# Two-layer graph network on one Trainium2 core: the opening loads in another order, one of them in another buffer, and other landing times in the plan

## The chip, the cores and the metric

The kernel runs on one core of one Trainium2 chip. The metric is device time in microseconds (us), lower is better. Beside the timed runs there is one profiled execution, from which every duration below is taken.

## What is computed

The input `x` holds 64 graphs of 256 nodes with 256 features, `adj` their 256 x 256 adjacency matrices (int32). Two layers follow each other.

```
# layer 0, with g = gat(h, W, a):
#   Wh = h @ W; e = leaky_relu(Wh @ a[:256] + (Wh @ a[256:]).T, 0.2)
#   g  = softmax(where(adj > 0, e, -9e15), axis=1) @ Wh
h = gat(gat(x, W1, a1), W2, a2)
h = layernorm(x + h, g_ln1, b_ln1)
x = layernorm(h + relu(h @ w_ff1 + b_ff1) @ w_ff2 + b_ff2, g_ln2, b_ln2)
# layer 1: eight heads of 32, attention weights masked by relation r and summed over r
A = softmax(q @ k.T / sqrt(32))
o = sum_r (A * (adj == r)) @ v_r
x = layernorm(x + o @ Wo + bo, g1, beta1)
x = layernorm(x + gelu(x @ W1 + b1) @ W2 + b2, g2, beta2)
```

Everything is fp32. The mask of layer 0 is 0 or 1, so that `adj` doubles as the mask of relation 1 in layer 1.

## The kernel before

The 64 graphs are worked on in 32 pairs. For each pair `whole_way` runs `gat_layers` (two graph attention layers), `feed_forward`, `attention` and a second `feed_forward`. Up to four pairs and a generator of one-time work, `reliefs` (it folds biases into each other and forms sums of weight blocks), are interleaved.

**A plan written by a simulator inside the kernel.** `run` keeps a clock for each engine (first values in `START`) and a time for each buffer (`free`). TensorE's work comes in steps that the generators yield, other engines' work in pieces handed over by `put` with a cost in us. The piece that could begin first is emitted, and `keep_order` ties each engine's instructions into that order. So the plan's guesses of when something lands change only the ORDER on each engine; what the chip waits for are the real semaphores. Loads that were issued before `run` starts enter the plan as fixed times: the dictionary `landed` (first normalisation's weights `ln0`, feed-forward weights `ff0` and `ff1`, `attention` weights) and the second argument of `load`.

**Engines work in order.** A DVE (VectorE) instruction that waits for a load holds everything behind it on DVE. SP (SyncE) issues nearly all loads, one queue, in order, and its waits hold the loads behind them too. The build gives each DMA one of eight completion semaphores in turn, so that SP issues a load only when the eighth load before it has landed.

**The opening.** Loads for the folded weight w12 come first (`W2`, `W1T`, `a2`, `a1c`). TensorE forms w12 (L127), DVE copies it out (L130). Then, for pair 0: products of `xT` with w12 (L528), evacuations (L520), exponentials (L451 to L453), transposes of their rows (L464) and copies (L467), attention weights `e` on DVE (L499, L501, L504), scaling of the node rows by the reciprocal sums on ACT (L509), the products of the first graph layer (L544), the same again for the second layer, with products L557. L570 adds the residual rows `x`, `layernorm` follows. The adjacency of a pair is read twice, by ACT, which makes bytes of it (L303, `small_adj`), and by DVE, which takes its maximum (L307, `largest`).

**Buffers.** `xT` and `adjT` share one buffer named `input`. For the first two pairs only, `adjT` goes into a buffer named `v` instead, which layer 1 uses later for its values: each of the two asks the pool for a tile `v` of which there is one, and takes half of it. The pool lets a new tile `v` be written when all readers of the one before have finished. `qk` is layer 1's buffer of queries and keys, also a single one.

**One-time work on DVE that waits for loads.** L899 adds a bias to each of three normalisation biases (`biased`), L901 subtracts weights (`differences`). The third addition of L899 reads `b_L_gnn_beta`, 42nd in SP's list. L912 and L921 are `reliefs`' products on TensorE, L340 the sums of weight blocks on DVE.

Of the kernel before, what the change touches and what calls it, by code (L numbers as in the profile page):

```python
# [10 lines left out]
F32 = mybir.dt.float32  # L11
# [7 lines left out]
P = 128  # L19
# [6 lines left out]
EVEN = 1e-37  # L26
HURRIED = 2
SLACK = 0.3
START = {"tensor": 8.5, "vector": 8.0, "scalar": 4.0, "gpsimd": 0.0, "sync": 32.0}


@with_exitstack
def two_layers(ctx: ExitStack, tc: tile.TileContext, t: dict, out: bass.AP, flag: bass.AP):
# [15 lines left out]
    KC = D // P  # L49
# [10 lines left out]
    io = ctx.enter_context(tc.tile_pool(name="io", bufs=1))  # L60
# [18 lines left out]
    def weights(name, pool=const):  # L79
        w = t[name]  # L80
        kc, m = w.shape[0] // P, w.shape[1]
        s = pool.tile([P, kc, m], F32, name="w_" + name)
        nc.sync.dma_start(s, w.rearrange("(c p) m -> p c m", p=P))
        return s
# [8 lines left out]
    def column(name):  # L93

        s = const.tile([P, t[name].shape[1]], F32, name="c_" + name)
        nc.sync.dma_start(s, t[name])
        return s

    work = ctx.enter_context(tc.tile_pool(name="work", bufs=1))
# [4 lines left out]
    def bank():  # L104
        return psum.tile([P, 512], F32, name="ps")
# [23 lines left out]
    for m in range(KC):  # L129
# [8 lines left out]
               "gpsimd": mybir.EngineType.Pool, "sync": mybir.EngineType.SP}  # L138
    clock = dict(START)
    waiting = {engine: [] for engine in engines if engine != "tensor"}  # L140
    alone = {}
    free = {name: [0.0] * n for name, n in (("bank", 8), ("a", 2 * HQ), ("m", 2 * HQ), ("h", 2 * HQ), ("yb", 1), ("yT", 2), ("yTa", 1),
                                             ("input", 1), ("rows", 1), ("e", 2), ("adj", 4), ("sums_yT", 1), ("sums_yTa", 1), ("x", 4))}
    table, moved = [None], [START["sync"]]

# [28 lines left out]
    def frees_at(time, names):  # L174
        for name in names:
            free[name].append(time)
# [9 lines left out]
    def takes(needs, count=1):  # L186
        for _ in range(count if needs else 0):
            free[needs].remove(min(free[needs]))

    def at_time(us):  # L190
        event = Event()
        event.time = us
        return event
# [83 lines left out]
        return slice(2 * b, 2 * b + 2)  # L277


    def load(pair, at=None):  # L280


        to, rows = {}, slice(2 * pair, 2 * pair + 2)

        def adjT():
            if at is not None:
                to["adjT"] = work.tile([P, 2, 2, 2 * D], F32, name="v")[:, pair].bitcast(I32).rearrange(
                    "p b (c n) -> p (b c) n", c=2)
            else:
                to["adjT"] = io.tile([P, 4, N], I32, name="input")  # L290
            nc.sync.dma_start(to["adjT"], t["adjT"][rows].rearrange("b (c p) n -> p (b c) n", p=P))

        def xT():
            to["xT"] = io.tile([P, KC, 512], F32, name="input")
            nc.sync.dma_start(to["xT"], t["xT"][pair].rearrange("(c p) b n -> p c (b n)", p=P))

        def x():
            to["x"] = io.tile([P, 4, D], F32, name="x", bufs=4)
            nc.sync.dma_start(to["x"], t["x"][rows].rearrange("b (c p) d -> p (b c) d", p=P))

        def small_adj():
            to["adj"] = io.tile([P, 4, N], U8, name="adj", bufs=4)
            nc.scalar.activation(to["adj"], to["adjT"], AF.Copy)  # L303

        def largest():
            to["empty"] = small.tile([P, 4], F32, name="empty", bufs=4)
            nc.vector.tensor_reduce(most[:, pair], to["adjT"].bitcast(U32), axis=AX.X, op=ALU.max)  # L307
            nc.vector.tensor_scalar(to["empty"], most[:, pair], 0.0, EVEN, ALU.is_le, ALU.mult)

        def in_bytes(there):  # L310
            return put("vector", 1.35, largest, put("scalar", 1.2, small_adj, there, needs="adj", rank=2), rank=2)

        def there(emit, *after, **more):
            return put("sync", 0.45, emit, *after, rank=3, lag=2.3, kb=512, **more)

        if at is None:
            adj = in_bytes(there(adjT, needs="input"))
            return to, [there(xT, adj), adj, there(x, needs="x")]
        takes("input", pair == 0)
        takes("x")  # L320
        for emit in (xT, adjT, x):
            emit()
        return to, [at_time(at), in_bytes(at_time(at)), at_time(at)]

    def first_weights(name, wide=None):

        w = t[name]
        rows = w.shape[1] // 2  # L330
        s = const.tile([P, 7, rows], F32, name="w_" + name)
        for c, at in ((0, (0, 2)), (1, (1, 6))):
            for half, n in enumerate(at):
                nc.sync.dma_start(s[:, n], w[c * P:(c + 1) * P, half * rows:(half + 1) * rows])
        return s
# [179 lines left out]
    def gat_layers(pair, to, loads):  # L515
        yield loads[:1], ["gat"], 2
        y = work.tile([P, 4, D + 4], F32, name="xw", bufs=2)

        def evacuated(to, k, wide, ps):
            return put("scalar", 0.4, lambda: nc.scalar.activation(to[:, k, :wide], ps[:, :wide], AF.Copy),  # L520
                       took(0.88), frees=["bank"])

        there = []
        for b in range(2):
            for j in range(2):
                k, ps = 2 * b + j, bank()
                for c in range(KC):
                    nc.tensor.matmul(ps[:, :D + 4], lhsT=to["xT"][:, c, k * P:(k + 1) * P], rhs=w12[:, c],  # L528
                                     start=c == 0, stop=c == KC - 1)
                there.append(evacuated(y, k, D + 4, ps))  # L530
            if b == 0:
                yield [], None, 2
        frees_at(clock["tensor"], ["input"] * (pair > 0))
        at_home, ratio, there = yield from addends(y, there, D + 2, 0, pair)
        e = [gat_weights(y, D + 2, at_home, ratio, [loads[1], *there], to, b) for b in range(2)]
        there = []
        for b in range(2):
            yield [e[b][1], *([] if b or not pair else [through_gat[pair - 1]])], None, 2
            if b == 0:
                z = work.tile([P, 4, D + 4], F32, name="xw", bufs=2)  # L540
            for i in range(2):
                ps = bank()
                for j in range(2):
                    nc.tensor.matmul(ps[:, :D + 2], lhsT=e[b][0]["e"][:, j, i * P:(i + 1) * P], rhs=y[:, 2 * b + j, :D + 2],  # L544
                                     start=j == 0, stop=j == 1)
                there.append(evacuated(z, 2 * b + i, D + 2, ps))
            frees_at(clock["tensor"], ["e"])
        done_with("gat")
        at_home, ratio, there = yield from addends(z, there, D, 1, pair)
        e = [gat_weights(z, D, at_home, ratio, there, to, b) for b in range(2)]  # L550
        normal = {}
        for b in range(2):
            yield [e[b][1], loads[2]], None, 1
            ps = bank()
            for i in range(2):
                for j in range(2):
                    nc.tensor.matmul(ps[:, i * D:(i + 1) * D], lhsT=e[b][0]["e"][:, j, i * P:(i + 1) * P],  # L557
                                     rhs=z[:, 2 * b + j, :D], start=j == 0, stop=j == 1)
            there = took(1.73)
            frees_at(there.time, ["e"])  # L560
            added = add_rows(to["x"], ps, b, there, loads[2])
            transposed(to["x"], layernorm(to["x"], ln[0], b, added, biased[0]), normal, b, pair, 0)
        happens(through_gat[pair], clock["tensor"])
        return normal
# [305 lines left out]
    def layernorm_weights(g, beta, more=None):  # L870
        if more:
            passing = work.tile([P, 2, 512], F32, name="ff", bufs=NF // 2)[:, 0, :D]
            v = t[more]
            nc.sync.dma_start(passing, bass.AP(tensor=v.tensor, offset=v.offset, ap=[[0, P], [1, D]]))
            more = passing, column(more + "c")
        return on_all(g, D), on_all(beta, D), more

    landed = {name: at_time(us) for name, us in (("ln0", 8.0), ("ff0", 15.0), ("attention", 30.0), ("ff1", 37.0))}
    loaded = {0: load(0, 6.5)}
    ln = [layernorm_weights("L0_gnn_g_ln1", "L0_gnn_b_ln1", "L0_gnn_b_ff2")]  # L880
    ff0 = (first_weights("L0_gnn_w_ff1p"), column("L0_gnn_b_ff1"), weights("L0_gnn_w_ff2"))
    loaded[1] = load(1, 18.0)
    ln.append(layernorm_weights("L0_gnn_g_ln2", "L0_gnn_b_ln2", "L1_gnn_bo"))

    wqk, wv = (const.tile([P, 7, D], F32, name=n) for n in ("wqk", "wv"))
# [11 lines left out]
    ff1 = (first_weights("L1_gnn_W1p"), column("L1_gnn_b1"), weights("L1_gnn_W2"))  # L897
# [502 lines left out]
```

## Time and profile before

| | us |
|---|---|
| four runs | 3042.93, 3044.46, 3045.43, 3047.18 |
| median | 3044.95 |
| profiled execution, its own time | 3047.15 |
| its span on the core | 3045.4 |

| engine | busy us | share of the span |
|---|---|---|
| TensorE matmul (PE) | 2997.9 | 98% |
| VectorE (DVE) | 2555.2 | 84% |
| ScalarE (ACT) | 1752.9 | 58% |
| GpSimd (POOL) | 253.6 | 8% |

PE is busy nearly throughout, in all slices of the span but the first and the last. So time is found or lost where PE is idle or its clock is lowered, and both happen in the first 65 us. The share of busy time over the whole span tells nothing of that stretch; it is read from the timeline, the chain of waits and windows of 2 us. `PEclk` in a window is the TensorE clock that was granted, 1.00 being full.

### The profile page before, as it was taken

The page shows a single profiled execution, that of the slowest core. Times are in us where ns is not written, and L with a number is a line of the kernel's source. Part 1 is how long each engine was busy: PE and PEld are TensorE (multiplying, and loading weights), DVE is VectorE, ACT ScalarE, POOL GpSimd, SP SyncE. Part 2 cuts the span into 40 slices and gives each one's busy share as a digit, 9 for nine tenths or more (in the row PEclk, how much of TensorE's full clock was granted, in tenths as well). Part 3 has the DMA queues.
Part 4 walks back from the last instruction along what each step waited for, and adds up shares of the span by engine and source line. Part 5 has one row for each costly group of instructions (what it writes and reads, how often), then busy time and mean ns, then how long its engine had stood idle before and what let it go on. Part 6 is the DMA issues. An engine that isn't in the chain of part 4 may idle for free.

```text
span 3045.4 us, 52870 instructions
## 1 busy us (share of the span) xinstructions
PE 2997.9 (98%) x19146; PEld 2454.6 (81%) x19146; DVE 2555.2 (84%) x5993; ACT 1752.9 (58%) x4096; POOL 253.6 (8%) x518
## 2 busy tenths in 40 slices
PE   7999999999999999999999999999999999999998
PEld 6887788878888888888888888888888888788876
DVE  5888988788988888888889888889888898888875
ACT  4556666556556555555565565565555655555654
POOL 0100010001100001100001000011000011000100
PEclk8999999999999999999999999999999999999999
DMA  6211141212212222112222112221122221122100
GB/s 182 77 47 60 35 125 56 70 57 82 69 42 67 77 84 77 53 53 70 84 84 77 39 60 77 84 77 61 50 69 80 84 77 52 54 70 70 50 1 22
DMA packets 211147, 205.76 MB, mean 68 GB/s; under 512 B 22336, under 2 KB 170432, under 8 KB 210880
## 3 DMA queue, kind: packets, MB, share of 16 engines
q1 hardware_dynamic: 210464, 202.06, 20.9%
q8 instruction: 153, 2.51, 0.3%
q14 instruction: 114, 0.93, 0.1%
q10 hardware_dynamic: 416, 0.26, 0.0%
HBM read 137.51 MB, written 64.73 MB: 66 GB/s over the span
## 4 chain that ended last, share of the span: by engine, by line
PE 68%; DVE 22%; DMA 5%; ACT 2%; issue 1%; SPq 1%; POOL 0%; DVEq 0%; ACTq 0%; POOLq 0%
PE ps L712 22%; PE ps L681 17%; PE ps L825 5%; PE ps L759 5%; PE ps L754 5%; DVE x L598 4%; PE ps L544 4%; PE ps L796 3%; DVE h L837 3%; PE ps L557 2%; DMA home<-yb 2%; PE ps L847 2%; DVE st L582 2%; DVE m L807 2%; PE ps L528 2%; DVE ff L392 2%
## 5 line engine op out<-in xcount | busy, mean ns | idle before, releaser
L712 PE MATMUL ps<-w_L_gnn_w_ff,ff 128*128 128x256 f32 x2048 | 470.9, 381 | 0.0
L712 PE MATMUL ps<-w_L_gnn_W,ff 128*128 128x256 f32 x2048 | 456.1, 380 | 1.8 <-ACT ff L693 1.8
L593 ACT ACTIVATE x<-x,less,rstd 128x256 f32<-128x256 f32 x512 | 279.1, 596 | 294.4 <-POOL less L589 294.2
L712 PEld LDWEIGHTS ps<-w_L_gnn_w_ff,ff 128*128 128x128 f32 x2048 | 386.6, 190 | 61.5 <-issue 9.8
L712 PEld LDWEIGHTS ps<-w_L_gnn_W,ff 128*128 128x128 f32 x2048 | 388.2, 190 | 57.6 <-ACT ff L693 2.6
L588 POOL TENSOR_TENSOR rstd<-rstd,mhalf 128x2 f32<-128x2 f32 x256 | 198.7, 776 | 2763.0 <-DVE less L585 2630.6
L807 DVE TENSOR_TENSOR m<-a,adj 128x512 f32<-128x512 f32 x512 | 349.0, 682 | 57.9 <-ACT a L803 57.9
L803 ACT ACTIVATE a<-ps 128x512 f32<-128x512 f32 x512 | 267.9, 603 | 222.9 <-PE ps L796 222.8
L681 PE MATMUL ps<-yT,w_L_gnn_W1p 128*128 128x256 f32 x1280 | 315.2, 382 | 4.7 <-ACT ff L687 2.4
L392 DVE TENSOR_TENSOR ff<-ps,ff 128x512 f32<-128x512 f32 x384 | 262.3, 684 | 65.6 <-PE ps L681 57.4
L681 PE MATMUL ps<-yT,w_L_gnn_w_ff1p 128*128 128x256 f32 x1280 | 307.5, 381 | 4.7 <-ACT ff L687 4.1
L687 ACT ACTIVATE ff<-ps 128x512 f32<-128x512 f32 x384 | 223.8, 590 | 98.1 <-PE ps L681 97.7
L681 PEld LDWEIGHTS ps<-yT,w_L_gnn_W1p 128*128 128x128 f32 x1280 | 240.2, 190 | 48.1 <-ACT ps L835 8.5
L681 PEld LDWEIGHTS ps<-yT,w_L_gnn_w_ff1p 128*128 128x128 f32 x1280 | 240.8, 190 | 46.8 <-ACT ff L687 14.3
L837 DVE RECIPROCAL h<-ps 128x256 f32<-128x256 f32 x128 | 223.3, 1745 | 21.6 <-PE ps L828 21.2
L509 ACT ACTIVATE xw<-xw,rs 128x258 f32<-128x258 f32 (+1 forms) x256 | 115.9, 502 | 201.6 <-DVE rs L504 201.5
L693 ACT ACTIVATE ff<-ff,c_L_gnn_b_ff 128x256 f32<-128x256 f32 x384 | 171.6, 504 | 94.4 <-DVE ff L392 94.2
L693 ACT ACTIVATE ff<-ff,c_L_gnn_b 128x256 f32<-128x256 f32 x384 | 173.2, 501 | 84.4 <-DVE ff L392 83.2
L811 DVE TENSOR_TENSOR h<-a 128x256 f32<-128x256 f32 x512 | 212.8, 416 | 0.0
L582 DVE BATCH_NORM_STATS2 st<-x 128x6 f32<-128x256 f32 x512 | 205.7, 402 | 0.9
L570 DVE TENSOR_TENSOR x<-ps,x 128x512 f32<-128x512 f32 x256 | 169.9, 680 | 16.2 <-PE ps L712 9.2
L769 ACT ACTIVATE qk<-ps,bqk 128x256 f32<-128x256 f32 x256 | 106.8, 469 | 111.3 <-PE ps L754 111.0
(128 smaller groups left out, 5011.2 us busy)
## 6 DMA issues: line engine op xcount, KB each, us to landing
home<-yb SPq DMA_DIRECT2D x182, 256.0 KB, 2.0
yT<-home SPq DMA_DIRECT2D x728, 64.0 KB, 2.0
rows<-row SPq DMA_DIRECT2D x60, 512.0 KB, 4.1
input<-in_xT SPq DMA_DIRECT2D x32, 512.0 KB, 4.8
x<-in_x SPq DMA_DIRECT2D x32, 512.0 KB, 4.0
out<-x SPq DMA_DIRECT2D x32, 512.0 KB, 5.1
input<-in_adjT SPq DMA_DIRECT2D x30, 512.0 KB, 4.4
v<-in_adjT SPq DMA_DIRECT2D x2, 512.0 KB, 6.8
```

The costliest lines, as they stand in the source:

```text
L392: nc.vector.tensor_tensor(self.target(c, h), self.bank[bank], self.target(c, h), ALU.add)
L582: nc.vector.bn_stats(st[:, j, :], rows[j])
L588: nc.gpsimd.tensor_tensor(rstd, rstd, mhalf[:, :2], ALU.pow)
L593: nc.scalar.activation(rows[j], rows[j], AF.Identity, bias=less[:, j:j + 1], scale=rstd[:, j:j + 1])
L681: nc.tensor.matmul(to, lhsT=w1[:, a, (t + slab) * P:(t + slab + 1) * P], rhs=b, **flags)
L687: return put("scalar", 0.5, lambda: nc.scalar.activation(target(c, h), blocks.bank["x"], AF.Copy), event, rank=-1)
L693: evacuated[h][m] = put("scalar", 0.4, lambda m=m, to=to, source=source: nc.scalar.activation(to, source, func, bias=b1[:, m:m + 1]), even ...
L712: nc.tensor.matmul(p2[:, j * D:(j + 1) * D], lhsT=f[m][:, (2 * j + b) * P:(2 * j + b + 1) * P], rhs=w2[:, m, :], start=m == 0, stop=m == N ...
L803: nc.scalar.activation(a[n][o], ps[o], AF.Exp)
L807: nc.vector.tensor_tensor(m[n][o], a[n][o], adj, ALU.mult)
L811: nc.vector.tensor_tensor(h[n][o], a[n][o][:, :N], a[n][o][:, N:], ALU.add)
L837: there = put("vector", 1.68, lambda: nc.vector.reciprocal(s, po[:, N:]), there, rank=0)
```

## The change

The first numbers of the plan change (`START`, `landed`, the arguments of `load`), which moves instructions on PE, DVE and ACT. In SP's queue the second pair's `xT` and `adjT` move ahead of the feed-forward weights, the two residual tiles `x` move behind them: `x` of pair 0 to just before `w_ff1p`, `x` of pair 1 to just after `w_ff2`. The second pair's `xT` is loaded into a tile `qk`, so that it no longer shares `input` with the first pair's. `x` is now emitted later than the rest of its load, by a list `rest`; each load has a time of its own in the plan.

```diff
-START = {"tensor": 8.5, "vector": 8.0, "scalar": 4.0, "gpsimd": 0.0, "sync": 32.0}
+START = {"tensor": 11.5, "vector": 11.5, "scalar": 4.0, "gpsimd": 0.0, "sync": 36.0}
...
+    rest = []
...
         def xT():
-            to["xT"] = io.tile([P, KC, 512], F32, name="input")
+            if at is not None and pair == 1:
+                to["xT"] = work.tile([P, 2, KC, 512], F32, name="qk")[:, 0]
+            else:
+                to["xT"] = io.tile([P, KC, 512], F32, name="input")
...
-        for emit in (xT, adjT, x):
+        for emit in (xT, adjT):
             emit()
-        return to, [at_time(at), in_bytes(at_time(at)), at_time(at)]
+        rest.append(x)
+        return to, [at_time(at[0]), in_bytes(at_time(at[1])), at_time(at[2])]
...
-        frees_at(clock["tensor"], ["input"] * (pair > 0))
+        frees_at(clock["tensor"], ["input"] * (pair != 1))
...
-    landed = {name: at_time(us) for name, us in (("ln0", 8.0), ("ff0", 15.0), ("attention", 30.0), ("ff1", 37.0))}
-    loaded = {0: load(0, 6.5)}
+    landed = {name: at_time(us) for name, us in (("ln0", 13.0), ("ff0", 23.0), ("attention", 35.0), ("ff1", 41.0))}
+    loaded = {0: load(0, (8.0, 9.5, 16.0))}
     ln = [layernorm_weights("L0_gnn_g_ln1", "L0_gnn_b_ln1", "L0_gnn_b_ff2")]
+    loaded[1] = load(1, (14.0, 15.5, 25.0))
+    rest[0]()
     ff0 = (first_weights("L0_gnn_w_ff1p"), column("L0_gnn_b_ff1"), weights("L0_gnn_w_ff2"))
-    loaded[1] = load(1, 18.0)
+    rest[1]()
```

## The prediction

> **What bounds the kernel now.** I read the page first. PE is busy 98% of the span; only its first slice (76 us) is thin. So at most what is lost in that slice can come back.
>
> ```profile
> span 3045.4 us, 52870 instructions
> PE   7999999999999999999999999999999999999998
> PEclk8999999999999999999999999999999999999999
> ```
>
> Second, the chain of waits in order of time, for the first 140 us: it names what PE waited for.
>
> ```profile
> 6.65 5.25 PE ps L127 x16
> 11.90 5.47 PE ps L528 x16
> ...
> 34.67 5.95 DMA b_L_gnn_beta<-in_L_gnn_beta
> ...
> 40.72 0.43 DVE b_L_gnn_beta L899
> ...
> 45.05 5.97 PE ps L557 x16
> 51.02 0.87 PE ps L464 x8
> 51.89 1.68 PE ps L912 x16
> 53.57 1.83 PE ps L921 x8
> 55.41 3.46 PE ps L912 x32
> 58.87 5.28 PE ps L544 x16
> ```
>
> From 45.05 on the chain stays on PE without a break. Before that it hangs on the load of beta, issued at 34.67 and landed 5.95 us later, at 40.62: DVE stands in L899 for it, pair 0's second weights `e` (L499) stand behind L899, and PE's L557 behind these. PE idles from 35.44 to 45.05 (9.6 us).
>
> Third, the timeline around the moved loads, and windows of 2 us for the DMA engines (columns: PE, PEld, DVE, ACT, POOL busy with counts, granted clock, DMA share, GB/s).
>
> ```profile
> 11.94 0.43 DVE L130 COPY w<-ps 128x260 f32<-128x260 f32 x1 [0.42 <-PE ps L127]
> 14.94 1.21 DVE L307 TENSOR_REDUCE most<-v 128x4 f32<-128x1024 uint32 x1
> 17.39 0.38 SPq L295 DMA_DIRECT2D input<-in_xT  x1
> 48.79 1.06 ACT L303 ACTIVATE adj<-input 128x1024 uint8<-128x1024 int32 x1 [2.28 <-DMA input<-in_adjT]
> ```
>
> ```profile
> 14.00:16.00 2.00, 2.00 (x7) 1.58 (x6) 1.40 (x2) 0.65 (x2) 0.00 (x0) 1.00 0.89 280
> 16.00:18.00 2.00, 1.35 (x7) 0.83 (x5) 0.49 (x3) 0.96 (x3) 0.00 (x0) 1.00 0.99 326
> 48.00:50.00 2.00, 2.00 (x7) 1.59 (x7) 1.14 (x2) 1.06 (x1) 0.00 (x0) 0.59 1.08 343
> ```
>
> SP did wait for the shared `input` buffer: its last issue before ended at 14.60, the next began at 17.39. But the DMA engines were 0.89 to 0.99 busy in that time, on 2 MB of feed-forward weights issued earlier. That wait cost the stream no bytes.
>
> **The change, part by part.**
>
> *The new order and a wait that stays.* `xT` of pair 1 no longer waits. Right behind it comes `adjT` of pair 1, and that still asks for the single buffer `v`, so it waits until ACT's L303 and DVE's L307 have read pair 0's. In before this cost nothing: L307 ended at 16.15, the issue came at 17.87. Now SP reaches it at about 7.5 (the issue of `xT` waits until `a1c` has landed, 7.05). L307 of pair 0 stands right behind L130 on DVE after the change, and L130 ends at 12.37; L307 lasts 1.21, so SP is held until 13.65, some 6 us. Queued behind it on SP: `x` of pair 0, `w_ff1p` x4, `b_ff1`, `w_ff2`, `x` of pair 1, and all that follows.
>
> What is lost is less than 6 us, since loads issued earlier still run. Up to the third broadcast of the first normalisation (landed 14.58) the stream moved 2688 KB; after the change the same sum, with `xT` of pair 1 for `x` of pair 0, so it has run dry at about 14.5. `adjT` then goes out into an empty queue. The rows for that: 512 KB landed 3.8 us after issue at 50.75, 3.7 at 77.54, 3.8 at 70.92. That gives 13.65 + 3.77 = 17.4. In before the 3588 KB from `w_ff1p` to `x` of pair 1 landed between 14.58 and 25.32, 334 KB per us; its first 512 KB count as landed at 14.58 + 1.53 = 16.1. The same 3588 KB are now 17.4 - 16.1 = 1.3 us late: `x` of pair 1 lands at 26.6. Bounds: if the remaining 3076 KB run at 380 KB per us (512 KB between the landings of `xT`, 8.34, and `adjT`, 9.69), they end at 25.5, 0.2 late; at the 280 of window 14 to 16, at 28.4, 3.1 late.
>
> [...]
>
> *From there to beta.* List and semaphore turns are the same from `x` of pair 1 on (each issue waits for the eighth load before it), so beta keeps its distance of 40.62 - 25.32 = 15.3 and lands at 41.9. This stretch is slow for its own reasons (small loads; one SP issue at 27.87 took 1.50 where most take 0.43). If that long issue does not recur, 1.1 comes back. So the lateness is +1.3, between -1.1 and +3.1.
>
> *The plan's later times.* They do not move `e` ahead of the wait: in the changed order DVE still has L899 with beta, then L901, then L499. What comes sooner before it is therefore wasted: ACT no longer stands until 24.03 for `adjT` of pair 1 ahead of the first L509, and L544 can begin up to 1 us before 25.54, but its results meet the same wait with 5 us to spare. That slack also covers the later `w_ff1p` (about 22 instead of 17.26) under L912; without it, up to 4.7 us would show.
>
> *A new wait on ACT.* After the change ACT does the two L509 of graph 0, then L303 of pair 2, then the two L509 of graph 1; before, L303 came last. L303 needs `adjT` of pair 2, which landed at 48.76 behind a saturated stream (343 to 374 GB/s from 40 to 50) and so keeps its distance to beta. L557 for graph 0 and, new in between, L464 fit into the wait. Behind L303 (48.79 + 1.06 = 49.85) one L509 takes 0.45, then PE has half of L557: 1.73 at full clock (so at 75.21 and 79.53). In before's times: 49.85 + 0.05 + 0.45 + 0.06 + 1.73 = 52.15 against 51.02. L464 (0.87) is already done then, leaving 1.68 + 1.83 + 3.46 = 6.97 to L544: 59.1 against 58.87, so +0.2. If the clock is still half, L557's half takes 2.98 (5.97 / 2) and it is +1.45.
>
> The row for the clock: PE resumed at 45.05, the window 48 to 50 was granted 0.59, the next 1.00. [...]
>
> *The stretch to the first feed-forward.* Before: 5.28 + 1.01 + 1.95 + 1.01 + 1.02 + 1.76 = 12.03 from L544 to L681 (70.89). After, L544 is split and all L528 come before the second transposes: about 1.74 x 2 + 1.45 for the half clock to 63.3, 1.01, 3.51, 1.01, 1.02 = 11.5; then ACT has the four L467 (needing L464) ahead of the last copy L653 (0.60), so PE waits 1.1: 12.6. That is +0.6. From about 110 us on the instructions stand in the same order on PE, and PE has no idle time to give back.
>
> *Sum.* 1.3 + 0.2 + 0.6 = +2.1 us. The profiled execution (3047.15, span 3045.4) would become 3049.3; on the median, 2.2 below it, 3047.0. That is 0.07%, within the 0.2% (6.1 us) that a measurement of this kernel can tell from no change.
>
> **The rivals.**
>
> Forecast, 0.56: SP is held until 13.65, about +2, no change that can be told.
>
> The freed queue, 0.23: the 2.79 us that SP waited for `input` come through, or the long issue vanishes; beta lands 1.1 to 2.8 earlier. For it: the wait is real in before. Against: DMA was 0.89 to 0.99 busy in it, and `v` holds the queue instead. -2.8 + 0.8 = -2.0 gives 3042.9. Also within 0.2%.
>
> Beta stops mattering, 0.05: `e` starts when its rows are ready (36.6 instead of 41.4, -4.8), and the clock does not fall (half of 3.4, -1.7), with `adjT` of pair 2 as early. -6.5 + 0.8 = -5.7, 3039.3; only a little more would pass 3038.9. Against it: beta is still in front on DVE.
>
> Slower, 0.16: `adjT` of pair 2 comes late enough that L303 holds graph 1's L509, and PE with it. The stream restarts at 13.65 and does not catch up: from 26.6 on it runs with short queues, at 156 GB/s from 24 to 40, and 3 us more there and half clock add up to 1.3 + 3 + 1.45 + 0.6 = 6.4, 3051.3. It decides when `adjT` of pair 2 lands after 54.1 (48.76 + 5.3) at full clock, after 52.8 at half.
>
> Range: lateness -1.1 and +3.1 with +0.8, or +2.05 at half clock, give 3044.7 to 3050.1; the runs scatter by 2 us, and the freed queue reaches down to 3042.9. I take 3042.5 to 3051.0. Faster by over 0.2%: 0.05; within: 0.79; slower: 0.16.
>
> **What would show it.** Right: no SP issue between `xT` of pair 1 (about 7.1) and `adjT` of pair 1 at 13.6 to 13.8, that load landing at 17.4; beta at 41 to 43; ACT's L303 of pair 2 standing between two pairs of L509 after a wait of several us; PE idle from about 35 to 46, and again for 1 us before L681. Wrong: `adjT` of pair 1 issued before 10 us; beta landed before 39 or after 45; PE idle before L557 shorter than 7 us; order differences that idle PE behind 75 us.

## The result, and the profile after

| | before | after |
|---|---|---|
| median, us | 3043.55 (51 runs) | 3049.25 (31 runs) |
| lowest to highest, us | 3041.27 to 3047.95 | 3045.55 to 3053.03 |
| profiled execution, us | 3047.15 | 3047.31 |
| its span, us | 3045.4 | 3045.5 |

The ratio of after to before is 1.0017, 95% interval 1.0012 to 1.0022: slower by 5.2 us (between 3.7 and 6.7), by the difference of the medians 5.7. That is below the 0.2% that the prediction took as the least that can be told, and inside its range; the direction was right, the size (+2.1 us) less than half. With this many runs the change can be told, which the forecast did not expect.

The two profiled executions differ by 0.16 us where the medians differ by 5.7: that of before lies 3.6 us above its median, that of after 1.9 below. So the loss cannot be read from the spans. It has to be read from the opening, up to a fixed piece of work, and from several executions.

SP's part of the timeline of after shows the hold that the prediction named, and ACT's the new wait:

```profile
7.36 0.38 SPq L300 DMA_DIRECT2D qk<-in_xT  x1
13.85 0.38 SPq L293 DMA_DIRECT2D v<-in_adjT  x1
...
50.50 1.06 ACT L308 ACTIVATE adj<-input 128x1024 uint8<-128x1024 int32 x1 [3.30 <-DMA input<-in_adjT]
```

SP issues nothing between 7.74 and 13.85. Line numbers are 5 higher than before for the two reads of an adjacency (L303 is L308, L307 is L312), 6 higher for the layers (L509 is L515, L544 is L550, L557 is L563, L681 is L687), 8 higher for `biased` and `reliefs` (L899 is L907, L912 is L920). The chain of waits of after:

```profile
12.23 0.43 DVE w L130
12.66 1.14 DVE most L312
...
13.85 0.38 SPq L293
...
17.84 10.18 DMA x<-in_x
...
36.33 6.09 DMA b_L_gnn_beta<-in_L_gnn_beta
...
42.51 0.42 DVE b_L_gnn_beta L907
...
46.85 3.78 PE ps L563 x8
50.63 1.71 PE ps L470 x8
52.34 1.96 PE ps L563 x8
...
70.98 1.21 ACT rows L473 x4
72.19 0.50 ACT yT L659
...
72.74 3.72 PE ps L687 x16
```

`x` of pair 1, queued behind the held load, now lands at 28.02 (25.32 before), beta at 42.42 (40.62), `adjT` of pair 2 at 50.47 (48.76). PE resumes at 46.85 (45.05). Then the chain, which before stayed on PE from 45.05 on, leaves PE once more for ACT before L687. TensorE's own timeline of after has two further stops behind that:

```profile
72.74 2.86 PE L687 MATMUL ps<-yT,w_L_gnn_w_ff1p 128*128 128x256 f32 x12 [1.14 <-ACT yT L659]
127.58 1.78 PE L687 MATMUL ps<-yT,w_L_gnn_w_ff1p 128*128 128x256 f32 x7 [0.25 <-ACT ff L693]
153.36 1.13 PE L760 MATMUL ps<-sums_yTa,wqk 128*128 128x256 f32 x4 [0.35 <-DVE qk L398]
```

In before PE has no idle time in any of these three places:

```profile
70.73 2.75 PE L681 MATMUL ps<-yT,w_L_gnn_w_ff1p 128*128 128x256 f32 x12
...
125.70 2.11 PE L681 MATMUL ps<-yT,w_L_gnn_w_ff1p 128*128 128x256 f32 x9
...
151.89 1.03 PE L754 MATMUL ps<-sums_yTa,wqk 128*128 128x256 f32 x4
```

From its first feed-forward matmul to its 720th matmul record (counted from 0 over the whole execution) before takes 80.30 us, after 81.59. With L687 starting at 72.74 instead of 70.73, after is 3.3 us behind at that record (154.33 against 151.03). Later the order on PE is the same in both, and what executions differ by there does not tell the kernels apart: from that record to the last matmul after takes 2879.8 us, a second execution of after (e4 below) 2882.9, before 2882.9, a second execution of before (e8) 2881.8. At that record itself the two executions of before stand 1.2 us apart.

### The profile page after: what moved, and what is told of

Its sections match the earlier page's. It is cut to its first block, busy times and chain, and to the rows that moved or that the text cites. A ratio compares the mean times of both kernels' runs of the same rounds, so it can differ in the third digit from the quotient of the medians.

```text
span 3045.5 us, 52872 instructions
## 1 busy us (share of the span) xinstructions
PE 3000.5 (99%) x19146; PEld 2457.6 (81%) x19146; DVE 2555.9 (84%) x5993; ACT 1751.4 (58%) x4096; POOL 253.4 (8%) x518
## 4 chain that ended last, share of the span: by engine, by line
PE 71%; DVE 20%; DMA 4%; ACT 2%; SPq 1%; issue 1%; POOL 0%; DVEq 0%; ACTq 0%; POOLq 0%
PE ps L718 22%; PE ps L687 17%; PE ps L831 5%; PE ps L765 5%; PE ps L760 5%; PE ps L802 4%; DVE x L604 3%; PE ps L550 3%; DVE h L843 3%; PE ps L853 2%; PE ps L563 2%; PE ps L534 2%; DVE st L588 2%; DVE m L813 2%; DMA home<-yb 2%; DVE ff L398 2%
## 5 line engine op out<-in xcount | busy, mean ns | idle before, releaser
L687 PE MATMUL ps<-yT,w_L_gnn_W1p 128*128 128x256 f32 x1280 | 315.2, 382 | 4.7 <-ACT ff L693 2.4
L687 PE MATMUL ps<-yT,w_L_gnn_w_ff1p 128*128 128x256 f32 x1280 | 307.3, 381 | 4.9 <-ACT ff L693 3.0
L687 PEld LDWEIGHTS ps<-yT,w_L_gnn_W1p 128*128 128x128 f32 x1280 | 240.2, 190 | 48.1 <-ACT ps L841 8.5
L687 PEld LDWEIGHTS ps<-yT,w_L_gnn_w_ff1p 128*128 128x128 f32 x1280 | 240.8, 190 | 46.8 <-ACT ff L693 12.5
L515 ACT ACTIVATE xw<-xw,rs 128x258 f32<-128x258 f32 (+1 forms) x256 | 116.3, 503 | 196.1 <-DVE rs L510 196.0
```

What stands on the lines that cost most here:

```text
L687: nc.tensor.matmul(to, lhsT=w1[:, a, (t + slab) * P:(t + slab + 1) * P], rhs=b, **flags)
```

## The experiments

Each ratio is to before, measured beside the experiment. "Stretch" is from the first feed-forward matmul (L681, L687) to the 720th matmul record.

**Taking the change apart: e1 to e4.** Theory: the loads and the plan's numbers each cost a few us, and they add. Rivals: all of it is the order, or all of it the loads.

e1 keeps before's plan numbers and changes loads and buffers only (its order on PE, DVE and ACT is before's):

```diff
-START = {"tensor": 11.5, "vector": 11.5, "scalar": 4.0, "gpsimd": 0.0, "sync": 36.0}
+START = {"tensor": 8.5, "vector": 8.0, "scalar": 4.0, "gpsimd": 0.0, "sync": 32.0}
-    ... ("ln0", 13.0), ("ff0", 23.0), ("attention", 35.0), ("ff1", 41.0)
+    ... ("ln0", 8.0), ("ff0", 15.0), ("attention", 30.0), ("ff1", 37.0)
-    loaded = {0: load(0, (8.0, 9.5, 16.0))}
+    loaded = {0: load(0, (6.5, 6.5, 6.5))}
-    loaded[1] = load(1, (14.0, 15.5, 25.0))
+    loaded[1] = load(1, (18.0, 18.0, 18.0))
```

> The changed kernel's load order and buffers with the plan's old numbers: every engine but SP keeps the order of the kernel before. Theory A (the queue is held by the buffer v, and the beta load and all behind it come late): SP issues adjT of pair 1 at about 13.8, beta lands at 42.0 to 42.6 instead of 40.6, PE resumes with L557 that much later, and the run is 1.5 to 2.0 us above before. Theory B (only the new order on the engines costs time): the late loads are covered, 0 to +0.5 us. Theory C (the loads cost everything): +5 to +6 us.

e2 is the opposite: before's loads and buffers with after's numbers in `START`, `landed` and `load` (its order on PE, DVE and ACT is after's).

> The kernel before with the changed plan numbers only: loads as before, every engine but SP in the order of the changed kernel. Theory A: beta lands at 40.6 as before; ACT stands for adjT of pair 1 (24.0) ahead of the first exponentials, which takes L544 some 4 us later but still ends near the beta wait (+0.6); L303 of pair 2 between the L509 pairs costs +0.2 to 1.5 and L653 behind L467 +0.6: +1 to +3 us in all. Theory B: nearly the whole loss of the changed kernel, +4.5 to +6 us. Theory C: 0.

e3 is after, with `adjT` of pair 1 in a tile that is free at that time, so that SP is not held:

```diff
-                to["adjT"] = work.tile([P, 2, 2, 2 * D], F32, name="v")[:, pair]...
+                tile = work.tile([P, 2, KC, N], F32, name="yTa") if pair == 1 else work.tile([P, 2, 2, 2 * D], F32, name="v")[:, 0]
...
```

> The changed kernel, but adjT of pair 1 goes into the buffer yTa, which nothing uses before layer 1, so that SP waits for no buffer in the opening; orders on all engines stay. Theory A: adjT of pair 1 is issued at about 7.8 and lands before 16, beta lands at 40 to 41, and of the loss of the changed kernel 1.3 to 2.5 us come back (+3 to +4.5 against before). Theory B: no change to the changed kernel (+5 to +6). Theory C: about the time of before (0 to +1).

e4 is after once more, unchanged.

> The changed kernel once more, for a second profile and beside the others on the same chip: +4 to +7 us against before. [...]

| | median | ratio | beta landed | PE resumes | L681/L687 | stretch |
|---|---|---|---|---|---|---|
| e1, loads alone | 3048.26 | 1.0007 [0.9998, 1.0016] | 42.25 | 46.67 | 71.21 | 80.31 |
| e2, plan alone | 3048.52 | 1.0010 [1.0001, 1.0019] | 39.63 | 46.96 | 72.98 | 81.60 |
| e3, SP not held | 3047.03 | 1.0004 [0.9995, 1.0013] | 39.66 | 44.09 | 73.11 | 81.61 |
| e4, after again | 3049.96 | 1.0016 [1.0007, 1.0025] | 40.96 | 45.38 | 73.37 | 81.60 |
| before, beside them | 3045.88 | | | | | |

Medians: loads +2.4, plan +2.6, both together +4.1; by the ratios 2.1, 3.0 and 4.9. The sum fits, but the times alone do not rule the rivals out: e1's interval holds both 1.000 ("all order") and 1.0016 ("all loads"), and e2's holds 1.0016 and just misses 1.000. Nor does e2 show the order's share as it is in after. With the old loads this order makes ACT stand for `adjT` of pair 1 (landed at 23.29) ahead of the first exponentials; PE idles 7.20 us before L464 and resumes with L557 late although beta had landed at 39.63. After has no such delay, so the good fit is in part a coincidence.

The split rests on the traces. e8, e1 and after run at full clock from 52.7 us on at the latest: at the 720th record e8 (before) stands at 149.87, e1, with the same order and the new loads, at 151.52, and after, with the new loads and the new order, at 154.33. By these three executions the loads cost 1.7 us and the order 2.8. The order's mark is exact: e2 has the old loads, and the same three stops as after, in its TensorE timeline:

```profile
24.71 1.94 PE L464 MATMUL ps<-ident,rise 128*128 128x128 f32 x8 [7.20 <-ACT rise L451]
...
46.96 3.78 PE L557 MATMUL ps<-xw,e 128*128 128x256 f32 x8 [4.33 <-ACT xw L509]
...
72.98 2.86 PE L681 MATMUL ps<-yT,w_L_gnn_w_ff1p 128*128 128x256 f32 x12 [1.14 <-ACT yT L653]
127.83 1.35 PE L681 MATMUL ps<-yT,w_L_gnn_w_ff1p 128*128 128x256 f32 x5 [0.26 <-ACT ff L687]
153.62 1.13 PE L754 MATMUL ps<-sums_yTa,wqk 128*128 128x256 f32 x4 [0.36 <-DVE qk L392]
```

In these eight executions the stretch has two values: 81.59 to 81.61 in the four traces with after's order, 80.30 to 80.31 in the four with before's (before, e1, and e5 and e8 below). In e3 SP goes straight on:

```profile
7.60 0.38 SPq L301 DMA_DIRECT2D qk<-in_xT  x1
8.03 0.47 SPq L294 DMA_DIRECT2D yTa<-in_adjT  x1
```

and beta lands 1.3 to 2.8 us earlier than with the hold. Its time, +1.2 us (between -1.5 and +4.0), came out below the +3 to +4.5 expected, although its trace carries the whole mark of after's order; the interval is too wide to tell which holds.

**Undoing the place of L303: e5.** After, with `adjT` of pair 2 planned 2 us later, which puts L308 behind all four L515 and restores before's order on PE:

```diff
-            adj = in_bytes(there(adjT, needs="input"))
+            adj = in_bytes(there(adjT, needs="input", lag=4.3 if pair == 2 else 2.3))
```

> The changed kernel with one number of the plan more: the load of pair 2's adjT counts as landing 2 us later in the plan. ACT's L303 of pair 2 then stands behind all four L509, and PE gets back the order of the kernel before; loads as in the changed kernel. Theory A (two costs, the held queue and the place of L303 with the order that follows it): the order's share, about 3 us, comes back, so +1 to +3 us against before; no PE idle time ahead of the first feed-forward; the feed-forward stretch to the 720th matmul record takes 80.3 us as in before and not 81.6. Rival (the later landing times as a whole cost, not the place of L303): still +4 to +6 us.

3048.02 beside 3045.28, ratio 1.0005 [0.9996, 1.0014]: as e1 (1.0007). beta landed at 42.42, late as in after; the stop before L687 is gone, L687 starts at 71.67, and the stretch is 80.31. So the order's cost hangs on where the plan puts one early read of an adjacency, as the trace shows (the interval of the time alone still overlaps that of e4); the loads' part stays.

**Taking beta off the path: e6 and e7.** e6 is before, with the plan told that the third bias addition can be done from 45 us on; DVE then does it behind `e`:

```diff
-    ... ("attention", 30.0), ("ff1", 37.0)
+    ... ("attention", 30.0), ("ff1", 37.0), ("ln2", 45.0)
-              for gbm, name in zip(ln, ("ln0", "attention", "attention"))]
+              for gbm, name in zip(ln, ("ln0", "attention", "ln2"))]
```

> The kernel before, but the addition that needs beta is planned for 45 us, so that DVE does pair 0's second weights e ahead of it. Theory A (the beta load sets when PE resumes): PE resumes with L557 at 39.5 to 41 instead of 45.05, the next bound is adjT of pair 2 (48.8) under L303 and the rows behind it; L544 of pair 1 starts near 55 instead of 58.9 and the run is 3 to 5 us below before. Rival (adjT of pair 2 takes over as the bound at once): 0 to -1.5 us.

e7 is e3 with before's numbers in the plan and the same edit.

> The load order of the changed kernel with adjT of pair 1 in the unused buffer yTa, the plan's old numbers, and the addition that needs beta planned for 45 us: no queue held, and beta out of the way. Theory A: L544 of pair 0 starts at about 24.6 instead of 25.5, all loads about 1 us earlier than in before, PE resumes at about 39 to 40, and the run is 4 to 6 us below before, the best of all. Rival (the load order brings nothing once the queue is free): the same as the kernel with beta late alone, -3 to -5 us.

e8 is before, unchanged, one profiled execution.

> The kernel before once more, for a second profile. [...]

| | median | ratio | PE resumes | second L544/L551 | record 720 |
|---|---|---|---|---|---|
| e6 | 3044.30 | 0.9998 [0.9989, 1.0007] | 39.95 | 56.21 | 148.96 |
| e7 | 3043.64 | 0.9993 [0.9984, 1.0002] | 38.89 | 55.13 | 148.16 |
| e8, before | 3044.81 (one run) | | 45.17 | 59.26 | 149.87 |
| before, beside them | 3045.28 | | | | |

In e6 PE resumes 5.2 us earlier than in e8, and the median moves by 1.0 us, which the interval does not tell from nothing. The place where the rest went is one line of DVE's timeline of e6:

```profile
49.28 1.22 DVE L307 TENSOR_REDUCE most<-input 128x4 f32<-128x1024 uint32 x1 [5.03 <-DMA input<-in_adjT]
```

DVE, relieved of one wait for a load, runs into the next one: L307 of pair 2 waits for `adjT` of pair 2 (landed 49.26), and pair 1's `e` stand behind it. A wait taken off an engine that works in order was replaced by the next one, some 9 us later. e7 shows the same: `adjT` of pair 2 landed at 48.17, L551 started at 55.13, and the median moved by 1.6 us where 4 to 6 had been expected.

**Moving that one as well: e9 and e10.** e9 is e6 with `adjT` of pair 2 planned 4 us later (`lag=6.3` in the line of e5); loads and buffers are before's. e10 is e7 with the same edit.

> Before, with the plan told that the third broadcast (beta) lands at 45 and that adjT of pair 2 lands 4 us later than planned. With beta alone planned late, PE resumed L557 at 39.95 instead of about 45, but DVE's next instruction, L307 of pair 2, then idled 5.03 us for adjT of pair 2 (landed 49.26), with pair 1's e behind it, and L544 started at 56.21. Here the built order has L307 of pair 2 behind those e. Theory: adjT of pair 2 is the wait that took beta's place; with L307 moved, L544 starts at 51 to 53.5, L681 at 65 to 66.5 instead of 68.74, and the time falls by about 3 us against beta alone: 3041.5 beside a before of 3045 (0.9985 to 0.999). Rival: L307 later also frees the input buffer later, xT of pair 2 is issued later and L528 of pair 2 waits for it: L681 at 68 or later and no gain (1.000, within 1 us of beta alone).

> The loads of after with adjT of pair 1 in a tile of its own (nothing holds SP), before's plan numbers, beta planned at 45 and adjT of pair 2 planned 4 us later. The kernel with the same loads and beta alone had L544 at 55.13, L681 at 67.93, and 3043.64 beside 3045.28. Theory (adjT of pair 2 is the next wait): L544 at 50 to 52.5, L681 at 64 to 66, 3040.5 beside 3045 (0.998 to 0.999). Rival (xT of pair 2 is the wait behind that one): L681 at 67 or later and 3043 to 3044.

e9: 3041.37 beside 3045.94, ratio 0.9985 [0.9976, 0.9994]. e10: 3041.61, 0.9986 [0.9977, 0.9995]. Both are faster than before with intervals that leave out 1, by 4.6 and 4.3 us. In e9's TensorE timeline one idle stretch is left between 40 and 76 us, and work runs through from there:

```profile
40.52 5.41 PE L557 MATMUL ps<-xw,e 128*128 128x256 f32 x16 [4.33 <-ACT xw L509]
...
53.64 1.99 PE L544 MATMUL ps<-xw,e 128*128 128x258 f32 x8
...
60.44 2.75 PE L681 MATMUL ps<-yT,w_L_gnn_w_ff1p 128*128 128x256 f32 x12
...
63.90 3.67 PE L528 MATMUL ps<-w,input 128*128 128x260 f32 x16
```

L544 starts at 53.64, 2.6 earlier than in e6, just past the 53.5 expected; no wait for `xT` of pair 2 appears in front of L528 (the rival), although its load went out 7.3 us later than in e6 (57.86; landed 61.73). L681 at 60.44 is far below the 65 to 66.5 expected only because the plan now puts it ahead of L528 of pair 2, so it isn't comparable. Nor is the 720th record, since this edit changes the order on PE as far as 426 us, with a stop of 0.53 us at 135.38 on the way. At record 2600, where the order is the same again, e9 is at 424.50, e6 at 425.59, e8 at 426.84 and before at 427.95: 1.1 us ahead of e6 and 2.3 to 3.5 ahead of before. So the opening accounts for part of the 4.6 us (interval 1.8 to 7.3), and the trace does not show the rest. e10, with loads in the new order, no hold and e9's order on PE, has no gain over e9 in the median (0.7 us at record 2600): once no early instruction waits for beta or for `adjT` of pair 2, landing 0.4 to 0.6 us sooner buys nothing that was measured.

## Why the prediction was right, and where its sum was not

**The hold on SP: right.** It said that SP reaches `adjT` of pair 1 at about 7.5 and is held by L307 until 13.65, landing at 17.4. After: 13.85 and 17.80; e1, e4, e5: 14.16, 12.74, 13.89, landing at 17.97, 17.10, 17.70. e3 shows that the hold is the tile: with another tile the issue is at 8.03. The 3.94, 3.81, 4.36 and 3.81 us from issue to landing stand beside the rows' 3.7 to 3.8.

**The lateness of beta, +1.3: right mechanism, a little small, and its landing right by luck.** Beta landed at 40.96 to 42.42 in the four traces with the hold, mean 42.0 (41.9 was said). Two misses cancel in that: `x` of pair 1 landed at 26.8 to 28.0, mean 27.5 (26.6 was said), and beta followed it after 14.1 to 15.1 us, mean 14.5, not after the 15.3 that it was said to keep. The other end was off: in five traces with before's loads beta lands at 39.63 to 40.74, mean 40.3, and the prediction took the 40.62 of a single one. So the term is +1.7. e1, which has only this term, measured +2.1, between -0.6 and +4.9.

**The new wait on ACT, +0.2: right in place, probably too small; the full clock that it took was wrong in after.** L308 stood between the pairs of L515 after 3.30 us of waiting, and `adjT` of pair 2 kept its distance to beta (8.05 us; 8.14 before). The full clock was the author's choice of two values. By the prediction's times PE would idle between the two halves of L557; in after it did not, since the clock was half there (0.50 from 46 to 52): the first half of L563 took 3.78 and L470, which fills the time between the halves, 1.71. In e4 and e3 PE did idle there, 0.43 and 0.98 us, and the chain of waits runs through `adjT` of pair 2 and ACT, as the prediction drew it. The windows of after (same columns as in the prediction):

```profile
46.00:48.00 2.00, 1.15 (x3) 0.97 (x4) 1.90 (x9) 0.91 (x2) 0.00 (x0) 0.50 1.10 349
...
50.00:52.00 2.00, 2.00 (x10) 1.74 (x8) 1.47 (x3) 1.50 (x3) 0.00 (x0) 0.50 1.04 331
```

From PE's resuming to the second L544 or L550 the four executions with before's order took 12.8 to 14.2 us (before 13.7, e8 14.1, e1 14.2, e5 12.8), the four with after's 14.3 to 15.0 (after 14.3, e4 14.8, e2 14.4, e3 15.0). The means are 0.9 apart. The order's share of this is not separable from the clock's: the half-rate stretch in there starts and ends elsewhere in each execution (it ended at 49.6 in before, 50.5 in e8, 52.6 in after). What an idle gap does to a rate that is still half was not shown: in e4 and e3 the full rate had returned before PE idled, at 50.75 and 47.07.

**The stretch to the first feed-forward, +0.6: right mechanism, half the size.** The stop before L687 was said to be 1.1 and is 1.14, and its cause is the one named, four L473 ahead of L659 on ACT. But the working set 12.6 with a half-clock surcharge against 12.03, and before's profiled execution had itself a half-rate stretch of 3.4 us in there (59.9 to 63.3). Like against like, at full clock throughout, the stretch is 10.31 (e1 and e8) and 11.61 (after and e2): +1.3.

**"From about 110 us on the instructions stand in the same order on PE, and PE has no idle time to give back": wrong, and the largest miss.** It was a term put at nothing. The order differs until about 160 us: pair 2 came through the opening at another time, and the plan placed the rest around it anew. After does both halves of L550 at 115.92 where before split L544 into 117.25 and 119.86; before does four L681 at 145.77 and at 151.03 that after does at 156.93 and 160.38. That cost 1.29 us, the two values of the stretch. It is made of the two stops shown above, where TensorE's next matmul starts 0.42 and 0.51 us late (the profile books 0.25 and 0.35 as idle), and of four matmuls there that each took 0.10 us longer than the others of their kind (before has one such, of 0.07). After's chain of waits shows what is short in those places: from 111.8 to 127.6 and from 138.4 to 153.4 it runs mostly over DVE, where before's is on PE throughout.

```profile
111.80 0.49 DVE e L505
...
126.95 0.58 ACT ff L693
...
127.58 2.98 PE ps L687 x12
...
152.70 0.61 DVE qk L398
```

An engine at 98% busy is not immune: it needs its inputs in the order in which it asks for them.

**Two of its signs of being wrong came true.** One is the idle time behind 75 us just told. The other: PE idled 6.30 us before L563 in after and 6.41 in e4, where less than 7 was to count against it. The idle time was not shortened by an earlier end: PE came to it later. L550 was to begin up to 1 us before 25.54 and began at 29.39, because L920 stood 1.36 and 0.96 us for `w_ff1p` and thirty of its matmuls took 6.56 us at half clock (all 32 took 3.93 before). The slack that the prediction named covered this, and beta still came last.

**The sum.** 1.7 + 0.2 + 1.3 + 1.3 = 4.5, against 2.1 said; with the 0.9 of the means in place of 0.2 it is 5.2. Measured were 5.2 by the ratio and 5.7 by the medians (3.7 to 6.7), and 4.9 and 4.1 the second time (e4). What is left is within the intervals. So the direction and the hold came out as argued; that the measured time lies inside the range is owed to its width, since the largest miss, the order behind 110 us, was no part of it.

**The rivals.** The freed queue: no. Freeing the queue of its last hold (e3) brings beta only 0.6 forward from before's 40.3, not the 2.79 that SP waited in before; the DMA engines were indeed busy in that time. Beta stops mattering: not in after, where DVE still had L907 ahead of L505. In the experiments beta was taken off the path, and the price of -6.5 did not hold: -1.0 by beta alone, since `adjT` of pair 2 was next on DVE, and -4.6 with that moved too. Slower by `adjT` of pair 2 landing after 52.8: it landed at 50.47 and 49.77. The loss came near that rival's size (6.4) by another way, the order.

## What to carry to other kernels

When a change gives a planner new numbers, compare the order on every engine to the end of the last difference, not to the first stretch that looks alike, and compare stretches at the same clock. On an engine that works in order, list the waits for loads one after the other before pricing the removal of the first: here the first was worth about 1 us alone and 4.6 with the second, by two landing times in the plan and with no load moved. A load moved ahead in a queue still goes out only when its buffer has been read (here at 13.85, reached at about 7.7), and it holds the loads behind it until then.

## What the runs showed of the hardware

In the opening the granted clock was half in two or three stretches, and two executions of the same program had different ones: before 6.8, 10.2 and 3.4 us (from 22.3, 39.4 and 59.9), before again 6.8 and 10.2 (from 23.3 and 40.3); after 13.7 and 6.8 (from 21.9 and 45.8), after again 13.7, 6.8 and 3.4. The one of 3.4 us in before, over solid matmul work, cost 1.7 us: from the second L544 to L681 before took 12.00 with it, and before again, the same instructions, 10.31 with no half rate in there.

Full rate came back 2.98 us after PE resumed in e3 (44.09 to 47.07) and 5.8 us after it in after (46.85 to 52.6). What makes the difference was not shown.
